# Latent-attention masks as 32-by-32 tiles of TensorE

## The chip, the cores and the metric

The kernel runs on one core of a Trainium2 chip. The core has a matrix engine (TensorE, PE in the profile; its weight loads have a row of their own, PEld), a vector engine (DVE), an activation engine (ACT), a general engine (POOL) and a queue for transfers (SP). Matrix products are written to PSUM, which this program uses as eight banks of 128 partitions by 512 float32 values. The metric is the device time of one execution in microseconds: 1879.91 us, the median of three runs (1879.69 to 1884.78).

## The reference

`x` has 8 sequences of 512 tokens with 128 channels. Two feed-forward stages with local attention stand around one attention over a latent space:

```python
x = x + 0.5 * ffn(layernorm(x))            # two layers each: local attention and a gated MLP
x = x + latent_attention(layernorm(x))     # 16 heads of 8 channels, causal
x = x + 0.5 * ffn(layernorm(x))
```

What bears on the change is the middle line, for each of 8 sequences and 16 heads:

```python
attn = einsum('bhql,bkl->bhqk', q_lat, c_kv) / sqrt(hs)
causal = tril(ones((T, T), bool))
attn = softmax(where(causal, attn, -inf))
```

The mask acts inside the 128-by-128 blocks on the diagonal of the 512-by-512 scores; blocks above the diagonal are not computed at all.

## The kernel before

The program has three parts: `ffn("f0")`, `latent_attention()`, `ffn("f1")`. In the two feed-forward parts every instruction is dealt out by the planner `Plan`, which orders steps by written costs and ranks while the program is being built. `latent_attention()` is written out in order by hand, and `in_order` keeps PE in that order. Some latent work lies outside its own part: `latent_begins` (inside f0, the last steps) makes the maxima of sequence 0 and of two batches of sequence 1, and `latent_ends` (inside f1, the first steps) makes the sums of sequence 7.

**Heads.** Sixteen heads are laid out as 4 groups `g` of 32 partitions by 4 heads `j` along the free dimension. A head's queries and keys fill 8 of its 32 partitions, the ninth carries a row for the shift by the maximum, and the rest is zero. A score product therefore contracts over 32 partitions, `rows = quadrant(g)`, and gives 128 output partitions.

**Units.** A unit is one PSUM bank (128 by 512). `maximum_products` (lines 1281 to 1304) puts one or two query blocks of scores into a bank, and DVE takes the row maximum (`maximum`, lines 1310 and 1314). `sum_products` (lines 1337 to 1362) puts the transposed scores into a bank, and ACT takes the exponential (`sum_exponential`, line 1366). `MAXIMA` and `SUMS` list which blocks share a bank. One block of 512 columns fills a bank, or two blocks do whose columns add up to 512.

**Masks.** Each unit begins by writing the mask into its diagonal blocks through PE, and the score products accumulate on top. Four matmuls, one for each 32 rows `k` of a diagonal block, take a piece of `masks["rows_of"]` as the stationary matrix (32 rows by 128 columns, of which 32 columns are an identity and the rest zero) and a piece of `masks["causal"]` or `masks["causal_t"]` as the moving one (lines 1288 and 1346). A piece writes all 128 output partitions, and adds zero on 96 of them. Only the first piece clears the bank (`start=(k == 0)`). The products come next: lines 1297 and 1355, float32, which the machine runs as two passes of weight load and matmul each.

**Pairs.** In the hand-ordered part the loop goes over `b` (7 sequences), the 10 batches of `SUMS` and the 4 head groups `g`. Each turn makes one sum unit of group `g` and, where one is left, one maximum unit of the next sequence of group `(g + 2) % 4`; `by_turns` interleaves the two units' matmuls one by one. This is called a pair here. There are 280 pairs, 272 of them with both units. All eight banks are given out in turn (`unit_bank`). In `latent_begins` and `latent_ends` two units of the same kind, of neighbouring groups, stand together: 24 and 20 such groups.

**Between the pairs** stand the value products (line 1372: 28 times 16 products over 128 partitions that write 32 partitions each), the transposes of their results (line 1453), and the projections of later sequences (lines 1421, 1426, 1434), at four fixed places of each sequence.

At the start of the program POOL builds the constants: `ident`, `ident16`, two bands, and the three masks (lines 317 and 325).

Of the kernel before, what the change touches and what calls it, by code (L numbers as in the profile page):

```python
# [12 lines left out]
ALU = mybir.AluOpType  # L13
# [3 lines left out]
P = 128  # L17
# [171 lines left out]
def kernel(  # L189
# [97 lines left out]
    ident16 = const.tile([P, P], BF16, name="ident16")  # L287
# [4 lines left out]
    for first in (True, False):  # L292
        band = const.tile([P, P], BF16, name=f"band{int(first)}")
        nc.gpsimd.memset(band, 0.0)
        for half in (0, WIN):
            rows = band[half : half + WIN]
# [14 lines left out]
    def quadrant(g):  # L311
        return slice(32 * g, 32 * g + 32)

    masks = {}
    for name in ("rows_of", "causal", "causal_t"):
        masks[name] = const.tile([P, 4, P], BF16, name=name)
        nc.gpsimd.memset(masks[name], 0.0)
    for g in range(4):
        for name, pattern, sign, op, fill in (
            ("rows_of", [[-32, 4], [1, P]], -1, ALU.not_equal, 1.0),  # L320
            ("causal", [[32, 4], [-1, P]], 1, ALU.is_ge, MASKED),
            ("causal_t", [[-32, 4], [1, P]], -1, ALU.is_ge, MASKED),
        ):
            rows = masks[name][quadrant(g)]
            nc.gpsimd.affine_select(
                out=rows, in_=rows, pattern=pattern, compare_op=op, fill=fill, base=0,
                channel_multiplier=sign,
            )
# [79 lines left out]
    def ffn(tagname, last):  # L408
# [600 lines left out]
        def latent_begins():  # L1009
# [67 lines left out]
            for b, held in [(0, held) for held in MAXIMA] + [(1, held) for held in MAXIMA[:LEAD]]:  # L1077
                q, kk = head_slots["q", b], head_slots["k", b]
                m = maxima_of(b)
                for half in (0, 1):  # L1080
                    banks = [Slot(mm), Slot(mm)]
                    units = [
                        (2 * half + n, lambda n=n, banks=banks: banks[n].tile) for n in range(2)
                    ]
                    step(
                        "lm", PE, 1.3, k,
                        lambda b=b, held=held, units=units: by_turns(
                            [maximum_products(b, held, g, bank) for g, bank in units]
                        ),
                        [(q, "d"), (kk, "d")], banks, [q, kk] + banks, 0.1,  # L1090
                    )
                    for (g, bank), t in zip(units, banks):
                        step(
                            "lr", DVE, 0.63, k,
                            lambda m=m, held=held, g=g, bank=bank: maximum(m, held, g, bank()),
                            [t], [("max", b, g)], [t], 0.0,
                        )
# [8 lines left out]
        def latent_ends():  # L1106
# [46 lines left out]
            for held in SUMS:  # L1153
                tiles, needs, slots = {}, [], []
                for half in (0, 1):
                    bank = Slot(pairs)
                    hold = [Slot(r_pT), Slot(r_pT)] if half else [Slot(r_pr)]
                    step(
                        "ep", PE, 1.3, k,
                        lambda held=held, half=half, bank=bank: by_turns([  # L1160
                            sum_products(b, held, 2 * half + n, lambda n=n: bank[:, n])
                            for n in range(2)
                        ]),
                        [(q, "d"), (kk, "d")], [bank], [q, kk, bank], 0.1,
                    )

                    def exponentials_(half=half, bank=bank, hold=hold, tiles=tiles):
                        if half:
                            for n in range(2):
                                tiles[2 + n] = flat(hold[n].tile)  # L1170
                                sum_exponential(tiles[2 + n], bank[:, n])
                        else:
                            t = flat(hold[0].tile)
                            sum_exponential(t.rearrange("p (n w) -> p n w", n=2), bank.tile)
                            tiles[0], tiles[1] = t[:, :512], t[:, 512:]

                    step(
                        "ee", ACT, 1.1, k, exponentials_, [bank], [(bank, 1)], [bank] + hold, 0.1
                    )
                    needs.append((bank, 1))  # L1180
                    slots += hold
# [38 lines left out]
    def heads(name, b):  # L1220

        if name == "v":
            return head_slots["v", b % 2].tile.rearrange("p n (h d) -> p n h d", d=32)
        if b % 3 == 2:
            half = slice(0, B // 2) if name == "q" else slice(B // 2, B)
            return Y[:, half].rearrange("p b n c -> p b (n c)")
        return head_slots[name, b % 3].tile
# [53 lines left out]
    def maximum_products(b, held, g, bank):  # L1281
        rows = quadrant(g)
        qp, kp = heads("q", b), heads("k", b)
        i0 = held[0][0][0]
        blocks = bank().rearrange("p (n w) -> p n w", w=P)
        diag = {3: blocks[:, 3:], 2: blocks[:, 2:], 1: blocks[:, 1::2]}[i0]
        todo = [
            lambda k=k: nc.tensor.matmul(
                diag[:, :, 32 * k :], lhsT=masks["rows_of"][rows, k],
                rhs=masks["causal"][rows, k, 32 * k :].unsqueeze(1)  # L1290
                .to_broadcast([32, len(held), P - 32 * k]),
                start=(k == 0), stop=False, skip_group_check=True,
            )
            for k in range(4)
        ]
        todo += [
            lambda i=i, j=j, at=at, n=n: nc.tensor.matmul(  # L1297
                bank()[:, at : at + (i + 1) * P], lhsT=qp[rows, j, i * P : (i + 1) * P],
                rhs=kp[rows, j, : (i + 1) * P],
                start=False, stop=(n == len(held) - 1), skip_group_check=True,  # L1300
            )
            for n, ((i, j), at) in enumerate(held)
        ]
        return todo
# [32 lines left out]
    def sum_products(b, held, g, bank):  # L1337

        rows = quadrant(g)
        qp, kp = heads("q", b), heads("k", b)  # L1340
        c0 = held[0][0][0]

        blocks = bank().rearrange("p (n w) -> p n w", w=P)
        diag = {0: blocks[:, :1], 1: blocks[:, ::3], 2: blocks[:, ::2]}[c0]
        todo = [
            lambda cut=cut, k=k: nc.tensor.matmul(
                diag[:, :, :cut], lhsT=masks["rows_of"][rows, k],
                rhs=masks["causal_t"][rows, k, :cut].unsqueeze(1)
                .to_broadcast([32, len(held), cut]),
                start=(k == 0), stop=False, skip_group_check=True,  # L1350
            )
            for k, cut in enumerate((32, 64, 96, 128))
        ]
        todo += [
            lambda c=c, j=j, at=at, n=n: nc.tensor.matmul(  # L1355
                bank()[:, at : at + T - c * P],
                lhsT=kp[rows, j, c * P : (c + 1) * P], rhs=qp[rows, j, c * P :],
                start=False, stop=(n == len(held) - 1), skip_group_check=True,
            )
            for n, ((c, j), at) in enumerate(held)  # L1360
        ]
        return todo
# [32 lines left out]
    def latent_attention():  # L1395
# [75 lines left out]
        for b in range(B - 1):  # L1471
            parts = {}
            for s, held in enumerate(SUMS):
                other = ahead.pop(0) if ahead else None
                tiles = {}
                for half in (0, 1):
                    two = two_tiles()
                    for n in range(2):
                        g = 2 * half + n
                        bank = unit_bank(f"st_{b}")  # L1480
                        units = [sum_products(b, held, g, lambda bank=bank: bank)]
                        if other is not None:
                            mb, mheld = other
                            mbank = unit_bank(f"sc_{mb}")
                            units.append(
                                maximum_products(mb, mheld, (g + 2) % 4, lambda mbank=mbank: mbank)
                            )
                        by_turns([
                            [lambda ins=ins: in_order(ins()) for ins in unit] for unit in units
                        ])  # L1490
                        sum_exponential(two[n], bank)
                        tiles[g] = two[n]
                        if other is not None:
                            maximum(maxima_of(mb), mheld, (g + 2) % 4, mbank)
# [124 lines left out]
```

## Time and profile before

| What | Value |
|---|---|
| Median of three runs | 1879.91 us |
| Profiled execution, its own time | 1883.39 us |
| Its span, first to last instruction | 1881.6 us |
| PE, share of the span busy | 93% |
| PE weight loads | 63% |
| DVE / ACT / POOL | 73% / 74% / 53% |
| Mean granted TensorE clock | 0.98 |
| Latent part, all eight banks in turn | about 823 to 1108 us of the span |
| Mask matmuls, each with a weight load | 2560 |

A row of a group reads: line, engine, operation, written tile, read tiles, shape, count, then the time in which any of the group was busy, the mean of one in ns, and the idle time of the engine just before them with what ended it. For PE a shape such as `32*128 32x256 bf16` says: 32 rows by 128 columns of stationary matrix, and 256 columns streamed past it. A float32 matmul has two rows in the records, one for each pass. Ends of matmuls are modelled and several are in flight at once, so the starts tell the pace, and a PE that is busy all the time need not be at its peak. The clock that TensorE was granted is told for each stretch of time.

### The profile page before, as it was taken

Reading aid. Unit: us, or ns where it says so; the run is one execution under the profiler, and the core shown is the slowest. Engines: PE = TensorE matmul, PEld = TensorE weight load, DVE = VectorE, ACT = ScalarE, POOL = GpSimd, SP = SyncE. Lnnn points to the kernel's source line nnn. Section 1 sums busy time; section 2 is a strip of 40 time slices with the busy share of each in tenths; the row PEclk is TensorE's granted clock in tenths of the full one; section 3 lists DMA queues with packets and bytes.
Section 4 is the critical chain, followed back from the end, with each engine's and each line's share of the span. In section 5 each row is a group of like instructions: output and inputs, shape, how many; then the busy total and the mean of one; then the engine's idle time right before and its main releaser. Section 6 shows DMA issues by size and latency. Waiting matters only on the chain.

```text
span 1881.6 us, 50927 instructions
## 1 busy us (share of the span) xinstructions
PE 1757.7 (93%) x19860; PEld 1179.0 (63%) x19860; DVE 1373.7 (73%) x2884; ACT 1389.6 (74%) x3911; POOL 990.1 (53%) x1685
## 2 busy tenths in 40 slices
PE   4899999999999989899999998989999999999998
PEld 2556666666666666467777764666666666666665
DVE  6888887777777867666766746878877777777764
ACT  2888878888888777236666666878888788778885
POOL 5776766666666665100000005867766666666651
PEclk9999999999999999769999999999999999999999
DMA  3111111111111111000000000111111111111110
GB/s 105 45 38 30 29 24 24 24 27 24 24 24 30 24 24 22 26 10 19 15 16 15 15 3 18 27 23 25 26 25 27 24 25 29 30 29 35 29 33 24
DMA packets 51968, 50.04 MB, mean 27 GB/s; under 512 B 22758, under 2 KB 34704, under 8 KB 51728
## 3 DMA queue, kind: packets, MB, share of 16 engines
q1 hardware_dynamic: 51584, 46.00, 10.5%
q8 instruction: 158, 2.59, 0.6%
q14 instruction: 82, 0.67, 0.1%
q10 hardware_dynamic: 144, 0.79, 0.1%
HBM read 6.30 MB, written 2.10 MB: 4 GB/s over the span
## 4 chain that ended last, share of the span: by engine, by line
PE 56%; DVE 18%; ACT 14%; POOL 6%; issue 4%; DMA 1%; SPq 1%; ACTq 0%; DVEq 0%; POOLq 0%
PE mm_f L542 9%; PE mm_f L504 8%; ACT pr_f L692 5%; PE mm_f L849 5%; PE st L1355 4%; PE mm_f L891 4%; PE mm_f L758 4%; PE mm_f L782 3%; PE lo L1372 3%; PE sc L1297 3%; DVE c_f L552 3%; DVE s_f L555 3%; PE sc_f L675 3%; ACT sq_f L568 2%; PE mm_f L1297 2%
## 5 line engine op out<-in xcount | busy, mean ns | idle before, releaser
L692 ACT ACTIVATE pr_f<-sc_f,nm_f,q_f 128x128 f32<-128x128 f32 x1024 | 460.3, 475 | 5.5 <-DVE nm_f L685 5.1
L542 PE MATMUL mm_f<-wqkv,hT_f 128*128 128x512 f32 x768 | 391.3, 613 | 30.4 <-DVE s_f L555 14.0
L576 POOL TENSOR_TENSOR qk_f<-c_f,s_f 128x512 f32<-128x512 f32 x256 | 325.0, 1274 | 115.1 <-DVE s_f L555 112.8
L700 POOL TENSOR_TENSOR pr_f<-pr_f,rso_f 128x512 f32<-128x512 f32 x256 | 266.0, 1040 | 220.8 <-DVE rso_f L716 180.7
L552 DVE TENSOR_TENSOR c_f<-mm_f,tab 128x512 f32<-128x512 f32 x256 | 175.3, 685 | 79.0 <-PE mm_f L542 34.6
L692 ACT ACTIVATION_READ_ACCUMULATOR pr_f<-sc_f,nm_f,q_f 128x1 f32 x1024 | 226.4, 221 | 0.0
L568 ACT ACTIVATE sq_f<-mm_f 128x512 f32<-128x512 f32 x256 | 153.1, 608 | 87.4 <-DVE s_f L555 61.4
L1366 ACT ACTIVATE pl<-st 128x512 f32<-128x512 f32 x280 | 152.8, 597 | 73.9 <-PE st L1355 59.8
L849 PE MATMUL mm_f<-fT_f,w 128*128 128x512 f32 (+1 forms) x384 | 190.5, 611 | 8.9 <-ACT ge_f L855 7.0
L504 PEld LDWEIGHTS mm_f<-ident,qk_f 128*128 128x128 f32 x1024 | 114.7, 141 | 128.9 <-POOL qk_f L612 52.1
L504 PE MATMUL mm_f<-ident,qk_f 128*128 128x128 f32 x1024 | 160.0, 280 | 31.8 <-POOL qk_f L612 12.8
L542 PEld LDWEIGHTS mm_f<-wqkv,hT_f 128*128 128x128 f32 x768 | 125.0, 192 | 99.1 <-issue 42.0
L684 DVE TENSOR_REDUCE nm_f<-sc_f 128x8 f32<-128x1024 f32 x128 | 155.3, 1214 | 42.6 <-PE sc_f L675 42.5
L758 PEld LDWEIGHTS mm_f<-pT_f,V_f 128*64 128x64 f32 (+1 forms) x4096 | 147.4, 136 | 60.2 <-issue 13.1
L758 PE MATMUL mm_f<-pT_f,V_f 128*64 128x64 f32 (+1 forms) x4096 | 179.8, 230 | 0.7 <-ACT pT_f L738 0.7
L555 DVE TENSOR_TENSOR s_f<-mm_f,tab 128x512 f32<-128x512 f32 x256 | 174.0, 680 | 0.0
L1387 POOL TENSOR_TENSOR X<-X,lon 128x128 f32<-128x128 f32 x26 | 11.9, 456 | 306.2 <-DVE lon L1381 306.2
L504 PE MATMUL mm_f<-ident,pr_f 128*128 128x128 f32 x1024 | 155.9, 280 | 11.5 <-DVE u_f L880 3.0
L504 PEld LDWEIGHTS mm_f<-ident,pr_f 128*128 128x128 f32 x1024 | 116.3, 142 | 74.1 <-POOL pr_f L700 33.0
L600 DVE TENSOR_REDUCE rn_f<-sq_f 128x16 f32<-128x1024 f32 x128 | 153.7, 1201 | 7.5 <-ACT sq_f L568 7.5
L782 PEld LDWEIGHTS mm_f<-wo,oT_f 128*128 128x128 f32 x1024 | 127.7, 191 | 43.0 <-ACT oT_f L771 18.1
L782 PE MATMUL mm_f<-wo,oT_f 128*128 128x128 f32 x1024 | 140.7, 280 | 3.2 <-ACT oT_f L771 2.9
(166 smaller groups left out, 3865.2 us busy)
## 6 DMA issues: line engine op xcount, KB each, us to landing
V_f<-V_f SPq DMA_DIRECT2D x224, 128.0 KB
hs_f<-Y SPq DMA_DIRECT2D x32, 112.0 KB
X<-in_x_dram SPq DMA_DIRECT2D x8, 256.0 KB
out_dram<-hs_f SPq DMA_DIRECT2D x8, 256.0 KB
Y<-fl SPq DMA_DIRECT2D x32, 32.0 KB
kT_f<-fl SPq DMA_DIRECT2D x32, 32.0 KB
V_f<-fl SPq DMA_DIRECT2D x32, 32.0 KB
wqkv<-in_wqkv_dram ACTq DMA_DIRECT2D x1, 768.0 KB
```

The costliest lines, as they stand in the source:

```text
L504: nc.tensor.transpose(dst[:, i * P : (i + 1) * P], src(i), ident)
L542: nc.tensor.matmul(ps.tile, lhsT=hT[:, i * P : (i + 1) * P], rhs=wqkv_sb[l][:, at * INNER : (at + 1) * INNER], start=True, stop=True,)
L552: nc.vector.tensor_mul(c1.tile, psv, tabs[l][:, 2 * s, i].unsqueeze(1).to_broadcast([P, H, DH]))
L555: nc.vector.tensor_mul(s1.tile.rearrange("p h (t d) -> p h t d", t=2), psv.rearrange("p h (t d) -> p h t d", t=2)[:, :, ::-1], tabs[l][:, ...
L568: lambda s=s, ps=ps: nc.scalar.activation(sq[:, s], ps.tile, AF.Square),
L576: lambda s=s, c1=c1, s1=s1: nc.gpsimd.tensor_add(qk[:, s].rearrange("p (h d) -> p h d", d=DH), c1.tile, s1.tile),
L684: nc.vector.tensor_reduce(nm.tile, sv, AX.X, ALU.max, negate=True)
L692: nc.scalar.activation(pr[:, h], sv[:, h % 2, h // 2], AF.Exp, bias=nm[:, h % 2, h // 2 : h // 2 + 1], scale=q8[:, h : h + 1], accum_out=s ...
L700: nc.gpsimd.tensor_mul(pr[:, heads], pr[:, heads], inv[:, heads].unsqueeze(2).to_broadcast([P, H // 2, P]),)
L758: nc.tensor.matmul(o[r * DH : (r + 1) * DH, u * P + w * WIN : u * P + (w + 1) * WIN], lhsT=(V2, V)[w][keys, i, h * DH : (h + 1) * DH], rhs ...
L782: nc.tensor.matmul(pw[:, :C], lhsT=oT[:, pr], rhs=wo_sb[l][:, pr], start=(pr == 0), stop=(pr == INNER // P - 1),)
L849: nc.tensor.matmul(ps[: hsz[c], :], lhsT=w1_sb[l][:, at + c * P : at + c * P + hsz[c]], rhs=fT.tile, start=True, stop=True,)
```

## The change

The stationary matrix of a mask piece becomes the 32-by-32 diagonal block of the bfloat16 identity (`ident16[rows, rows]`), and the piece writes only the 32 partitions that are its own (`diag[quadrant(k), ...]`). As the pieces no longer share partitions, each clears its own part of the bank (`start=True`). `masks["rows_of"]` and the POOL instructions that fill it are gone. The order of the instructions on PE, ACT and SP and the waits among them stay as they are; the number of matmuls and of weight loads stays too. DVE has the same work, with a few small instructions of one layer norm in another order.

```diff
-    for name in ("rows_of", "causal", "causal_t"):
+    for name in ("causal", "causal_t"):
         masks[name] = const.tile([P, 4, P], BF16, name=name)
         nc.gpsimd.memset(masks[name], 0.0)
     for g in range(4):
         for name, pattern, sign, op, fill in (
-            ("rows_of", [[-32, 4], [1, P]], -1, ALU.not_equal, 1.0),
...
             lambda k=k: nc.tensor.matmul(
-                diag[:, :, 32 * k :], lhsT=masks["rows_of"][rows, k],
+                diag[quadrant(k), :, 32 * k :], lhsT=ident16[rows, rows],
                 rhs=masks["causal"][rows, k, 32 * k :].unsqueeze(1)
                 .to_broadcast([32, len(held), P - 32 * k]),
-                start=(k == 0), stop=False, skip_group_check=True,
+                start=True, stop=False, skip_group_check=True,
             )
...
             lambda cut=cut, k=k: nc.tensor.matmul(
-                diag[:, :, :cut], lhsT=masks["rows_of"][rows, k],
+                diag[quadrant(k), :, :cut], lhsT=ident16[rows, rows],
                 rhs=masks["causal_t"][rows, k, :cut].unsqueeze(1)
                 .to_broadcast([32, len(held), cut]),
-                start=(k == 0), stop=False, skip_group_check=True,
+                start=True, stop=False, skip_group_check=True,
             )
```

## The prediction

> **What bounds the kernel now.** First the page, by slices, to see whether PE is at its limit where the masks are.
>
> ```profile
> PE   4899999999999989899999998989999999999998
> PEclk9999999999999999769999999999999999999999
> ```
>
> A slice is 47 us; the latent part is slices 17 to 24. PE is busy throughout, and the clock dips only in slices 17 and 18. Next, windows cut at the latent part's edges, then the value products (line 1372) alone in the long one.
>
> ```profile
> core 0: us, PE busy (x) PEld busy (x) DVE busy (x) ACT busy (x) POOL busy (x), PEclk, DMA share, GB/s
> 771.50:822.90 51.40, 47.60 (x363) 33.33 (x362) 38.21 (x92) 3.20 (x10) 1.80 (x1) 0.57 0.04 8
> 822.90:1108.50 285.60, 285.60 (x5077) 206.34 (x5076) 189.31 (x386) 183.03 (x337) 11.85 (x26) 0.99 0.05 15
> 1108.50:1143.40 34.90, 33.07 (x440) 18.06 (x435) 8.06 (x36) 23.30 (x39) 3.86 (x13) 1.00 0.01 2
> ...
> 822.90:1108.50 285.60, 65.48 (x886) 25.41 (x886) 0.99 0.05 15
> ```
>
> The same query by lines 1453, 1426, 1434, 1421 and 1325 gives 17.06, 11.90, 6.95, 4.39 and 2.09 us. With the 65.48 that is 107.9 us that belong to no pair; 285.6 - 107.9 = 177.7 us are left for 280 pairs, 0.635 us a pair. DVE's maxima stand 0.60 us apart, start to start, in every run of pairs (the timeline has 7 in 4.28 us), so a pair is now paced by DVE, with PE close behind.
>
> How PE does a pair in that time shows in the timeline (start, length, engine, line).
>
> ```profile
> 959.95 1.16 PE L1372 MATMUL lo<-pl,V_f 128*32 128x384 f32 x20
> 961.03 1.12 PE L1426 MATMUL pq<-xT,full_q 128*128 128x512 f32 x2
> 962.00 1.02 PE L1426 MATMUL pq<-xT,full_k 128*128 128x512 f32 x2
> 962.95 0.18 PE L1346 MATMUL st<-causal_t,rows_of 32*128 32x32 bf16 x1
> 962.96 0.28 PE L1288 MATMUL sc<-causal,rows_of 32*128 32x256 bf16 x1
> ...
> 963.12 0.64 PE L1355 MATMUL st<-kT_f,V_f 32*128 32x512 f32 x1
> ...
> 963.24 0.56 PE L1297 MATMUL sc<-V_f,kT_f 32*128 32x384 f32 x1
> 963.25 0.18 PE L1346 MATMUL st<-causal_t,rows_of 32*128 32x32 bf16 x1
> 963.25 0.28 PE L1288 MATMUL sc<-causal,rows_of 32*128 32x256 bf16 x1
> ...
> 963.60 0.59 PE L1355 MATMUL st<-kT_f,V_f 32*128 32x512 f32 x1
> ```
>
> Two readings carry the forecast. The second pair's masks start at 963.25, while the first pair's products (963.12 and 963.24) have just begun: as long as the shape is 32 rows by 128 columns, four row groups run side by side, two pairs at once. And where the shape changes, nothing overlaps. The weight-load rows at those places:
>
> ```profile
> 961.03 0.30 PEld L1426 LDWEIGHTS pq<-xT,full_q 128*128 128x128 f32 x2 [0.41 <-issue]
> ...
> 962.95 0.09 PEld L1346 LDWEIGHTS <-rows_of 32*128 32x128 bf16 x1 [0.76 <-issue]
> ```
>
> The value products end at 959.95 + 1.16 = 961.11 and the projections at 962.00 + 1.02 = 963.02; the next load starts 0.07 us before each end, though inside one shape a load starts beside the running matmul. I find the same 0.07 at every place in the trace where rows or columns go from one of 32, 64 and 128 to another, some 860 of them, also where only the columns change (128*128 to 128*32, 27 places). It leaves some 95 ns between the last streamed column and the next load.
>
> [...]
>
> **The change, part by part.**
>
> *Shape.* Masks become 32*32, products stay 32*128. Each pair, and each of the 24 + 20 groups outside, now has two changes of shape where it had none: into the masks, and into the products. This decides.
>
> *A pair after, at full clock.* Masks: two units' eight pieces go to eight different tiles. The nearest row is the local attention's own mask (line 665, four pieces of shape 64*64, 4 in 0.41 us with 0.40 each), so pieces start 3.5 ns apart; eight take 0.03. The last ends after 0.27 (256 columns, line 1346) and the products' load starts 0.07 earlier: 0.22 us. If column tiles of one row group did not run side by side, it would be as now, about 0.36. Products: the first load is no longer covered. In the projections at 961.03 the two passes start 0.53 apart behind a change and 0.43 apart elsewhere, so 0.107 is bare. The streams total 512 columns in two passes, 0.427 each: 0.853 (split units stream as much). Then 0.095 until the next pair's load. Sum 0.22 + 0.107 + 0.853 + 0.095 = 1.27 us, and the next pair can't start under it. Against 0.635: 280 x 0.635 = +178 us. With DVE at 0.60 and ACT at 0.60 a pair, PE alone now paces; their waits for PE grow, and none of them is late.
>
> *The clock.* It halves at 770.2 and at 787.3. What ran just before the second, 783.9 to 787.3, where two groups' maxima stand:
>
> ```profile
> L1297 PE MATMUL mm_f<-V_f,kT_f 32*128 32x512 f32 x8 | 2.4, 657 | 0.0
> L1288 PE MATMUL mm_f<-causal,rows_of 32*128 32x128 bf16 x4 | 0.8, 211 | 1.0 <-DVE lnm L1314 1.0
> ```
>
> Weighted by the share of the array's cells, 8 passes x 0.427 / 4 are 0.85 us, and 1280 mask columns at 0.43 ns / 4 are 0.14: 0.29 of the window. Counted so in 3.41 us windows over the whole trace, the clock falls after windows of 0.08 to 0.37, stays at 0.40 and more (once at 0.33), and comes back after 0.80 or more (not at 0.62). A pair after the change has 0.853 x 2 / 4 = 0.427 plus 0.03 of small masks in 1.27 us: 0.36, now about 0.8. So the stage comes to the edge of the clock. Windows with a value product in them are well above, windows of pairs alone vary from about 0.32 to 0.39. At half clock the streams and loads double: 0.33 + 0.213 + 1.707 + 0.095 = 2.34 us, +1.07 a pair, at 0.38 of the cells, so it stays down until the next value products (28 of them, 10 pairs apart). Bounds: 0 if it never falls; at the most three pairs in ten are at full clock behind each value product, 196 x 1.07 = 210, and a third of the other 108 us doubles, 35: +245. I take about the middle, 112 pairs at half: +120.
>
> *Groups outside.* In `latent_begins` the clock is 0.50; DVE's maxima (four starts, 789.75 to 795.00) put three groups in 5.25 us, 1.75 each. After: 2.34. Some 18 of the 24 stand back to back: +10 (0 to 14). In `latent_ends` 20 groups lie among other shapes; one alone costs 0.03 more, one that overlapped its neighbour 0.62: +6 (1 to 12).
>
> *Weight loads.* 2560 of 92 to 96 ns (128 columns) become 32 columns; the nearest row is line 1372's 32-column load, 109 ns. They lie beside matmuls except after a change of shape, where the first is in the 0.22. Bounds -13 to +16 ns a group: nothing. If the cover goes, 324 groups x 0.016 = 5 us.
>
> *Clearing and waits.* `start=True` on every piece is what line 665 does; no cost shows there. No wait is added or taken, on PE, ACT, SP or POOL.
>
> *POOL at the start.* One fill (0.47 start to start) and four selects (0.59) go, 2.8 us. The first layer norm's small steps start on POOL at 14.28 when its queue is empty, though their input was there at 8.54. So the first projections (18.44) come earlier, unless a load is late next: -3 (-3 to 0).
>
> *Sum*, against the profiled execution's 1883.4 us (span 1881.6 and 1.8 around it): +178 + 120 + 10 + 6 - 3 = +311, 2194. The median lies 3.5 lower: 2190.
>
> **Rivals.**
> 1. *The drain comes, the clock holds.* For it: one window at 0.33 did not drop it, and pairs alone average 0.36. Against: one low window is enough, and each stretch has several. 1880 + 178 + 13 = about 2070; with less bare time a pair (1.22) 2055.
> 2. *The drain holds back only the row group concerned.* For it: row groups of one shape run freely. Against: at 962.95 the load waits for the whole array, though there the array was one tile, so the trace doesn't decide. Two pairs overlap, 1.27 / 2 = 0.635: no change in the pairs, about 1880 to 1900.
> 3. *Other side: faster.* 32*32 beside 32*128 is no change of shape for the machine. Column tiles then shorten the masks and DVE alone paces: (0.635 - 0.600) x 280 = 10, and 3 at the start: 1867. It decides as soon as a pair takes less than 0.635. Against: 128*128 to 128*32 differs in columns alone and drains all 27 times.
>
> **How the numbers follow.** Forecast (drain, clock falls in a part) 0.62; rival 1 0.24; rival 2 0.07; rival 3 0.07. Rivals 2 and 3 are left out of the range. Low end: rival 1 at 1.22 a pair and the lower bounds, 1880 + 164 - 3 = 2041, so 2040. High end: 1880 + 178 + 245 + 14 + 12 - 3 = 2326, so 2320. Faster by over 0.3% (about what a measurement of this kernel tells from no change): rival 3, 0.07. Rival 2 is split: 0.03 same, 0.04 slower. Slower: 0.90.
>
> **What would show it.** Masks of 32*32 at 4 ns spacing; PEld loads of the products 0.07 us before the last mask's end; no mask start while a product runs; pair to pair 1.27 us at clock 1.0 and 2.34 at 0.5; DVE's maxima as far apart, with idle time put down to PE; the clock row below 9 in slices of the latent part; both feed-forward parts as long as before. Masks starting beside the other row groups' products, or maxima still 0.60 apart, would prove the drain wrong; a clock row of nines would prove the +120 wrong.

## The result and the profile after

The changed kernel takes 2286.11 us, the median of four runs (2272.50 to 2293.17), against 1881.21 us (1879.69 to 1884.78) for the kernel before: a ratio of 1.214, with a 95% interval of 1.2115 to 1.2166. The profiled execution is the shortest of the four, 2272.5 us with a span of 2270.7 us. It is 389.1 us longer than the span of before, and every figure below is taken from these two profiled executions.

All line numbers after the constants are one lower than before: masks L1345 and L1287, products L1354 and L1296, value products L1371. First the same two rows of the page by slices; a slice is now 57 us.

```profile
PE   5999999999999899999999999998999999999998
PEclk9999999999999856766676666689999999999999
```

The latent part is slices 14 to 27, fourteen where there were eight shorter ones, and the clock row is between 5 and 8 in all of them. Before, it dipped in two. The PE row gives no hint: it is at nines. The windows cut at the first mask of each stretch say how much each took, and the last row counts the value products (L1371) alone.

```profile
core 0: us, PE busy (x) PEld busy (x) DVE busy (x) ACT busy (x) POOL busy (x), PEclk, DMA share, GB/s
767.40:825.80 58.40, 55.29 (x362) 26.90 (x362) 38.12 (x92) 2.15 (x9) 1.80 (x1) 0.59 0.03 6
825.80:1496.00 670.20, 669.40 (x5095) 352.35 (x5094) 214.73 (x387) 198.16 (x338) 11.76 (x26) 0.66 0.02 6
1496.00:1529.50 33.50, 33.50 (x382) 15.55 (x380) 7.26 (x34) 21.48 (x35) 3.29 (x12) 1.00 0.01 2
...
825.80:1496.00 670.20, 104.16 (x896) 33.73 (x896) 0.66 0.02 6
```

Measured from mask to mask in the same way, the edges of the three stretches of before lie at 771.5, 822.9, 1111.4 and 1140.5 us. The long stretch of before reads:

```profile
822.90:1111.40 288.50, 287.77 (x5097) 207.73 (x5097) 189.57 (x387) 183.64 (x338) 11.85 (x26) 0.99 0.05 15
```

That gives the whole bill:

| Stretch | Before, us | After, us | Difference |
|---|---|---|---|
| Start to first maximum mask | 771.5 | 767.5 | -4.0 |
| `latent_begins`, first maximum mask to first sum mask | 51.4 | 58.4 | +7.0 |
| Hand-ordered part, to the first mask of `latent_ends` | 288.5 | 670.2 | +381.7 |
| `latent_ends`, first mask to last mask | 29.1 | 33.5 | +4.4 |
| Rest, to the end | 741.1 | 741.2 | 0 |

In the hand-ordered part PE is busy for 669.4 of 670.2 us. DVE's and ACT's busy times grow by only 25 and 15 us (189.6 to 214.7, and 183.6 to 198.2), and both now wait. Two groups of the page show on what; the last number of the mean is in ns, and behind the bar stand the idle time and what ended it.

```profile
L1365 ACT ACTIVATE pl<-st 128x512 f32<-128x512 f32 x280 | 167.2, 597 | 399.2 <-PE sc L1296 367.4
L1309 DVE TENSOR_REDUCE lnb<-sc 128x4 f32<-128x512 f32 x112 | 77.5, 692 | 210.7 <-PE sc L1296 210.7
```

The work itself still takes 597 and 692 ns. ACT waits 399 us ahead of its exponentials, nearly all for PE.

How a pair runs now is in PE's timeline. The clock falls at 961.95, so the pair whose masks start at 961.09 runs almost wholly at full clock and the next one at half (start, length, engine, line).

```profile
960.56 0.59 PE L1354 MATMUL st<-kT_f,V_f 32*128 32x512 f32 x1
960.78 0.38 PE L1296 MATMUL sc<-Y 32*128 32x128 f32 x2
961.09 0.20 PE L1345 MATMUL st<-causal_t,ident 32*32 32x64 bf16 x1
...
961.11 0.20 PE L1287 MATMUL sc<-causal,ident 32*32 32x64 bf16 x1
961.32 0.58 PE L1354 MATMUL st<-kT_f,V_f 32*128 32x384 f32 x1
...
962.40 0.41 PE L1296 MATMUL sc<-Y 32*128 32x128 f32 x1
962.75 0.23 PE L1345 MATMUL st<-causal_t,ident 32*32 32x64 bf16 x1
...
962.76 0.39 PE L1345 MATMUL st<-causal_t,ident 32*32 32x256 bf16 x1
962.77 0.23 PE L1287 MATMUL sc<-causal,ident 32*32 32x64 bf16 x1
963.08 1.00 PE L1354 MATMUL st<-kT_f,V_f 32*128 32x384 f32 x1
...
964.75 0.42 PE L1296 MATMUL sc<-Y 32*128 32x128 f32 x1
965.09 0.23 PE L1345 MATMUL st<-causal_t,ident 32*32 32x64 bf16 x1
```

Eight masks start within 0.02 us, so the column tiles do run side by side. Then nothing starts until they are through, the products run, and the next pair's masks start only when these are through: 961.09 to 962.75 to 965.09, 1.66 us across the fall of the clock and 2.34 us below it. The two pairs that overlapped before (masks at 962.95 and again at 963.25) no longer do. The weight loads at the two changes of shape:

```profile
963.08 0.28 PEld L1354 LDWEIGHTS st<-kT_f,V_f 32*128 32x128 f32 x1 [0.22 <-issue]
963.09 0.28 PEld L1296 LDWEIGHTS sc<-Y 32*128 32x128 f32 x1
...
965.09 0.10 PEld L1345 LDWEIGHTS <-ident 32*32 32x32 bf16 x1 [0.22 <-issue]
```

The last mask ends at 962.76 + 0.39 = 963.15 and the products' load starts 0.07 before; the last product ends at 964.75 + 0.42 = 965.17 and the load for the next masks starts some 0.07 before. The masks at 965.09 belong to other row groups than the products that end there, and still wait. These rows decide between the forecast and rival 2: the drain, the wait at a change of shape for all that still runs, takes the whole array. The trace of after has 605 changes between these two shapes, and at every one the load starts 71 to 73 ns before the last matmul's end.

DVE's maxima show the pair as a pace.

```profile
959.97 0.69 DVE L1309 TENSOR_REDUCE lnb<-sc 128x4 f32<-128x512 f32 x1 [3.13 <-PE sc L1296]
961.24 0.69 DVE L1309 TENSOR_REDUCE lnb<-sc 128x4 f32<-128x512 f32 x1 [0.58 <-PE sc L1296]
962.88 0.69 DVE L1309 TENSOR_REDUCE lnb<-sc 128x4 f32<-128x512 f32 x1 [0.95 <-PE sc L1296]
965.23 0.69 DVE L1309 TENSOR_REDUCE lnb<-sc 128x4 f32<-128x512 f32 x1 [1.66 <-PE sc L1296]
967.58 0.69 DVE L1309 TENSOR_REDUCE lnb<-sc 128x4 f32<-128x512 f32 x1 [1.65 <-PE sc L1296]
```

1.27 us from start to start at full clock, 2.35 at half. Over the part the median is 1.28 (88 intervals wholly at full clock) and 2.35 (131 wholly at half). Between 862.9 and 1494.4 the clock falls 27 times; it is typically full for 6.8 us and half for 10 to 24 us. Each time that it came back in this part, value products had run in the 3.5 us before.

### The profile page after: what moved, and what is told of

Its sections match the earlier page's. It is cut to its first block, busy times and chain, and to the rows that moved or that the text cites. A ratio compares the mean times of both kernels' runs of the same rounds, so it can differ in the third digit from the quotient of the medians.

```text
span 2270.7 us, 50918 instructions
## 1 busy us (share of the span) xinstructions
PE 2153.1 (95%) x19860; PEld 1317.2 (58%) x19860; DVE 1397.9 (62%) x2884; ACT 1401.9 (62%) x3911; POOL 985.3 (43%) x1680
## 4 chain that ended last, share of the span: by engine, by line
PE 66%; DVE 13%; ACT 10%; POOL 6%; issue 4%; DMA 1%; SPq 0%; ACTq 0%; DVEq 0%; POOLq 0%
PE st L1354 16%; PE mm_f L541 8%; PE mm_f L503 7%; PE mm_f L848 5%; PE lo L1371 5%; ACT pr_f L691 4%; PE sc L1296 4%; PE mm_f L890 3%; PE mm_f L757 3%; PE mm_f L781 3%; PE sc_f L674 2%; DVE c_f L551 2%; DVE s_f L554 2%; ACT sq_f L567 2%; PE mm_f L1296 2%
## 5 line engine op out<-in xcount | busy, mean ns | idle before, releaser
L1365 ACT ACTIVATE pl<-st 128x512 f32<-128x512 f32 x280 | 167.2, 597 | 399.2 <-PE sc L1296 367.4
L1354 PE MATMUL st<-kT_f,V_f 32*128 32x128 f32 (+3 forms) x640 | 324.0, 632 | 0.0
L1296 PE MATMUL sc<-V_f,kT_f 32*128 32x384 f32 (+3 forms) x624 | 315.2, 633 | 0.0
L1313 DVE TENSOR_REDUCE lnm<-sc 128x1 f32<-128x512 f32 (+1 forms) x160 | 110.7, 692 | 176.8 <-PE sc L1296 160.6
L1309 DVE TENSOR_REDUCE lnb<-sc 128x4 f32<-128x512 f32 x112 | 77.5, 692 | 210.7 <-PE sc L1296 210.7
L757 PEld LDWEIGHTS mm_f<-pT_f,V_f 128*64 128x64 f32 (+1 forms) x4096 | 147.4, 136 | 60.2 <-issue 14.1
L1354 PEld LDWEIGHTS st<-kT_f,V_f 32*128 32x128 f32 x640 | 142.0, 251 | 60.0 <-issue 34.1
```

The lines of the kernel that those rows point to most:

```text
L757: nc.tensor.matmul(o[r * DH : (r + 1) * DH, u * P + w * WIN : u * P + (w + 1) * WIN], lhsT=(V2, V)[w][keys, i, h * DH : (h + 1) * DH], rhs ...
L1296: lambda i=i, j=j, at=at, n=n: nc.tensor.matmul(bank()[:, at : at + (i + 1) * P], lhsT=qp[rows, j, i * P : (i + 1) * P], rhs=kp[rows, j, : ...
L1354: lambda c=c, j=j, at=at, n=n: nc.tensor.matmul(bank()[:, at : at + T - c * P], lhsT=kp[rows, j, c * P : (c + 1) * P], rhs=qp[rows, j, c * ...
```

## The experiments

The theory has two steps. Each change of shape makes TensorE wait until the whole array is empty, so that pairs no longer overlap; and the work that is left fills too few of the array's cells to hold the clock. The rivals: that small masks or clearing each piece cost the time by themselves, that the clock falls for another reason, that only the row group concerned waits.

### Half as many changes of shape

```diff
+                    units, read = [], []
                     for n in range(2):
                         g = 2 * half + n
                         bank = unit_bank(f"st_{b}")
-                        units = [sum_products(b, held, g, lambda bank=bank: bank)]
+                        units.append(sum_products(b, held, g, lambda bank=bank: bank))
+                        read.append(lambda n=n, bank=bank: sum_exponential(two[n], bank))
...
-                        by_turns([
-                            [lambda ins=ins: in_order(ins()) for ins in unit] for unit in units
-                        ])
-                        sum_exponential(two[n], bank)
...
+                    by_turns([
+                        [lambda ins=ins: in_order(ins()) for ins in unit] for unit in units
+                    ])
+                    for r in read:
+                        r()
```

The masks stay 32 by 32; the maxima of the two pairs are put into `read` in the same way. Four units instead of two stand between two changes of shape, in four different row groups.

> The changed kernel, with the masks of two pairs issued together and then the products of the two pairs, so that four units share the two changes of shape. Nothing else changes: the same pieces of 32 by 32, the same clearing, the same number of matmuls. Theory (each change of shape empties TensorE, and nothing overlaps across it): a group of two pairs takes 0.25 + 0.107 + 0.853 + 0.095 = 1.31 us in place of 2 x 1.28, 0.65 a pair, and the share of cells doubles to about 0.7, so the clock stays at 1.0 through the latent part. The hand-ordered part takes about 140 x 1.31 + 108 = 291 us against 288 before; the whole 1885 to 1925 us (some waits for banks included). Rival (the narrow pieces or their clearing are slow in themselves): as many pieces, so near 2286 us. Rival (the drain is of one row group alone): no gain from sharing, near 2286 us.

Measured: 1912.37 us (1903.57 to 1930.01), a ratio of 1.018 (1.0115 to 1.024). The windows from mask to mask:

```profile
768.60:828.00 59.40, 56.78 (x362) 27.40 (x362) 38.23 (x92) 2.03 (x9) 1.80 (x1) 0.56 0.03 6
828.00:1130.60 302.60, 301.21 (x5103) 172.10 (x5102) 198.62 (x387) 182.78 (x338) 11.92 (x26) 0.98 0.05 14
1130.60:1175.00 44.40, 44.40 (x389) 19.14 (x388) 7.24 (x33) 21.66 (x35) 3.31 (x12) 0.73 0.00 1
```

The hand-ordered part falls from 670.2 to 302.6 us with the same masks and the same matmuls. The clock is full from 837.8 to 1134.8 without a break, and maxima stand 0.61 us apart inside a group of two pairs and mostly 0.7 to 0.9 from group to group. So neither the small masks nor their clearing cost the time; where they stand does. Of the 36.6 us by which the span is still longer than before, 14.1 lie in this part, 8.0 in `latent_begins`, which was not regrouped, and 15.3 in `latent_ends`, in which the clock was at half from 1134.8 to 1158.7; the start is 2.9 earlier and the rest 2.1 longer.

The same grouping in the kernel before is the control:

> The kernel before, with the masks of two pairs together and then their products, as in the other run with two pairs; masks of 32 by 128. It tells what the grouping alone does. Theory: no change of shape stands between pairs here, so grouping has nothing to save: within 1% of before, 1865 to 1900 us. If the grouping itself were a gain, this run would be clearly below 1865.

Measured: 1887.95 us (1885.75 to 1889.20), 1.0036 (1.0024 to 1.0049), the hand-ordered part 294.7 us against 288.5.

```profile
821.90:1116.60 294.70, 290.64 (x5097) 187.02 (x5096) 194.81 (x387) 182.38 (x338) 11.86 (x26) 0.99 0.05 14
```

Grouping alone gains nothing, so what it gave the changed kernel was the changes of shape that it took away, and the clock with them.

### More work, at a higher clock

```diff
+                        spare = unit_bank(f"sp_{b}")
+                        idle = quadrant((g + 1) % 4)
+                        units.append([None] * 4 + [
+                            lambda spare=spare, idle=idle: nc.tensor.matmul(
+                                spare, lhsT=heads("k", b)[idle, 0, :P],
+                                rhs=heads("q", b)[idle, 0], start=True, stop=True,
+                            )
+                        ])
...
```

> The changed kernel, with one product more in each pair: 512 columns, float32, on a row group that is idle then, into a spare bank that nobody reads. It streams beside the pair's products and takes no time of its own, but adds 0.21 us of a quarter of the cells twice, 0.36 to about 0.52 of the cells. Theory (the clock follows the share of cells that stream): the clock stays at 1.0 in the latent part, pairs take 1.28 us throughout, and the whole takes about 1881 + 280 x 0.645 + 7 = 2065 us (2050 to 2090), some 220 us less than the changed kernel in spite of more work. Rival (the clock falls because of the empty stretches at each change of shape, which stay as they are): 2286 us or a little more.

Measured: 2085.83 us (2084.10 to 2087.55), 1.109 (1.1066 to 1.111): 200 us less than the changed kernel, with a product more in every pair. The windows of the whole hand-ordered part, and of the stretch in which the clock stayed full:

```profile
828.00:1311.90 483.90, 483.10 (x5657) 272.19 (x5656) 212.43 (x387) 198.09 (x338) 11.92 (x26) 0.95 0.03 9
865.20:1298.70 433.50, 433.50 (x5331) 246.72 (x5324) 200.34 (x360) 185.88 (x316) 11.92 (x26) 1.00 0.04 10
```

The clock is full for 433.5 us on end. The maxima there show the drain without the clock:

```profile
984.39 0.69 DVE L1313 TENSOR_REDUCE lnm<-sc 128x1 f32<-128x512 f32 x1 [0.60 <-PE sp L1490]
985.68 0.69 DVE L1313 TENSOR_REDUCE lnm<-sc 128x1 f32<-128x512 f32 x1 [0.60 <-PE sp L1490]
986.97 0.69 DVE L1313 TENSOR_REDUCE lnm<-sc 128x1 f32<-128x512 f32 x1 [0.60 <-PE sp L1490]
```

1.29 us a pair, twice what a pair took before, and the profile puts each maximum's wait down to the spare product of line 1490, the last to end. This run parts the two terms: the changes of shape keep the pair at 1.28, and the clock is what took the pairs of the changed kernel from 1.28 to their mean of 1.83. A share of cells explains it, 0.36 a pair without the spare product and (3 x 0.853 / 4 + 0.03) / 1.28 = 0.52 with it. Counted from the records in windows of 3.41 us, each pass's stream time weighted by its rows and columns over 128 x 128 (all times at full or half clock in this part are multiples of it: 3.4, 6.8, 10.2, 13.7 us and so on), the changed kernel's clock falls behind windows of 0.21 to 0.36 and holds behind windows from 0.35 up; with the spare product the windows of the full stretch are at 0.49 and more, but for its end, where one of 0.41 holds and one of 0.34 is followed by the fall. PE's busy time does not explain it: 669.4 of 670.2 us at clock 0.66, 483.1 of 483.9 at 0.95. Nor does PE's idle time: the changed kernel's part has 0.8 us of it in all, and the clock falls 27 times there.

### Half the pieces changed

```diff
-                diag[:, :, 32 * k :], lhsT=masks["rows_of"][rows, k],
+                diag[quadrant(k), :, 32 * k :], lhsT=ident16[rows, rows],
...
-                start=(k == 0), stop=False, skip_group_check=True,
+                start=True, stop=False, skip_group_check=True,
```

This is the kernel before with the change in the maximum units alone; the masks of the sum units stay at 128 columns.

> The kernel before with the change made to the maximum units alone; the sum units keep masks of 32 by 128. Since a pair interleaves the two units' pieces one by one, nearly every mask piece of a pair now follows one of the other shape. Theory (price per change of shape, 0.1 us behind each stream): the masks of a pair take their streams one after another, 1024 columns or 0.43 us, and 8 x 0.1 us, 1.23 in place of 0.22; a pair takes about 1.23 + 0.107 + 0.853 + 0.095 = 2.28 us at full clock, at 0.24 of the cells, so the clock falls as well, and a pair takes about 3.7 us at half clock. With a third of the pairs at full clock the whole is 1881 + about 750 = 2630 us (2400 to 2850). Rival (each changed piece costs something of its own): half of the pieces, half of the loss, near 2080 us.

Measured: 2658.84 us, a single execution, beside 1879.87 for the kernel before; it lies in the range of the theory.

```profile
829.40:1888.40 1059.00, 1058.24 (x5095) 540.39 (x5094) 215.00 (x387) 197.53 (x338) 11.75 (x26) 0.58 0.01 4
```

PE's timeline at full clock, where a pair's masks now go one by one:

```profile
963.02 0.18 PE L1346 MATMUL st<-causal_t,rows_of 32*128 32x32 bf16 x1
963.13 0.23 PE L1288 MATMUL sc<-causal,ident 32*32 32x128 bf16 x1
963.29 0.20 PE L1346 MATMUL st<-causal_t,rows_of 32*128 32x64 bf16 x1
...
963.99 0.18 PE L1288 MATMUL sc<-causal,ident 32*32 32x32 bf16 x1
964.10 0.69 PE L1355 MATMUL st<-kT_f,V_f 32*128 32x512 f32 x1
```

Half of the masks are small, and the loss is almost twice as large. In a pair the two units are interleaved piece by piece, so a 32-column mask now stands next to a 128-column one, and there are eight changes of shape to a pair instead of two (2176 in the trace, 272 pairs). Maxima stand 2.03 or 2.17 us apart at full clock (19 intervals, 2.28 expected) and mostly 3.5 to 3.77 at half. It is the changes that are paid for, not the small pieces.

### No change of shape at all

```diff
-            lambda i=i, j=j, at=at, n=n: nc.tensor.matmul(
-                bank()[:, at : at + (i + 1) * P], lhsT=qp[rows, j, i * P : (i + 1) * P],
+            lambda i=i, j=j, at=at, n=n, k=k: nc.tensor.matmul(
+                bank()[quadrant(k), at : at + (i + 1) * P],
+                lhsT=qp[rows, j, i * P + 32 * k : i * P + 32 * k + 32],
...
-            for n, ((i, j), at) in enumerate(held)
+            for n, ((i, j), at) in enumerate(held) for k in range(4)
```

The products of the sums are cut in the same way, so that everything in a unit is 32 by 32.

> The changed kernel, with the score products in the same shape as the masks: each product's stationary matrix is cut into four of 32 columns, and each piece writes its own 32 partitions. Four times as many product matmuls and loads, but no change of shape inside or between pairs. Theory (change of shape): pairs overlap again and DVE paces at 0.60 us; the masks' pieces run side by side, so PE needs less than before: 1865 to 1890 us. Rival (narrow pieces are slow in themselves): worse than the changed kernel, since there are more of them, above 2286 us.

Measured: 1969.40 us (1962.75 to 1971.92), 1.046 (1.0441 to 1.0486). The direction held, 317 us less than the changed kernel; the number did not.

```profile
817.60:1194.80 377.20, 373.87 (x10423) 255.10 (x10422) 209.98 (x387) 195.32 (x338) 11.84 (x26) 0.99 0.05 13
```

The clock is full but for the first microseconds, and a pair takes (377.2 - 109.0) / 280 = 0.96 us (109.0 us is what the lines that belong to no pair take in this part of the kernel before). PE's timeline has the next pair's masks beside the running products:

```profile
960.64 0.27 PE L1355 MATMUL st<-Y 32*32 32x128 f32 x1
960.66 0.20 PE L1346 MATMUL st<-causal_t,ident 32*32 32x64 bf16 x1
...
960.70 0.25 PE L1346 MATMUL st<-causal_t,ident 32*32 32x192 bf16 x1
960.73 0.37 PE L1296 MATMUL sc<-V_f,kT_f 32*32 32x256 f32 x1
...
961.02 0.21 PE L1287 MATMUL sc<-causal,ident 32*32 32x128 bf16 x1
```

With one shape the overlap is back, as the theory says. But the masks come in two portions, 0.3 us apart, at this place, and the pair is not at DVE's pace. Two more runs ask why. The first groups two pairs as above:

> The kernel in which products too are cut into pieces of 32 columns, now with the units of two pairs issued together, four row groups in turn. Question: why did the kernel with one shape everywhere take 0.99 us a pair and not 0.60. Theory (the pieces of one pair, some 34 matmuls with as many loads, fill the queue in front of TensorE while they wait for their own tiles, so the next pair's pieces for idle row groups come too late): with four row groups in turn the queue holds work for the whole array, a pair comes down to 0.60 to 0.65 us, and the whole to 1860 to 1895 us. Rival (a narrow piece is slow in itself, for its loads or for streams that disturb each other): as many pieces, so near 1969 us.

Measured: 1937.61 us (1936.05 to 1940.43), 1.031 (1.0294 to 1.0323). It fits neither expectation.

```profile
818.00:1167.30 349.30, 331.35 (x10431) 195.49 (x10430) 199.15 (x387) 182.49 (x338) 11.88 (x26) 1.00 0.05 14
```

Maxima stand 0.61 apart inside a group, with a gap behind it, and a pair takes (349.3 - 109.0) / 280 = 0.86 us. The second cuts into 64 columns, masks as well as products, and starts from the kernel before:

```diff
-                diag[:, :, 32 * k :], lhsT=masks["rows_of"][rows, k],
+                diag[half(k // 2), :, 32 * k :],
+                lhsT=masks["rows_of"][rows, k, half(k // 2)],
...
-                start=(k == 0), stop=False, skip_group_check=True,
+                start=(k % 2 == 0), stop=False, skip_group_check=True,
...
-                bank()[:, at : at + (i + 1) * P], lhsT=qp[rows, j, i * P : (i + 1) * P],
+                bank()[half(k), at : at + (i + 1) * P],
+                lhsT=qp[rows, j, i * P + 64 * k : i * P + 64 * k + 64],
```

Here `half(k)` is the range of 64 partitions from 64 k on, and a product becomes two; the sums are cut in the same way.

> The kernel before with every piece of a unit, masks and products, cut into tiles of 32 rows by 64 columns: no change of shape between masks and products, masks over half the partitions, twice as many products. It asks what kept the version with 32-column pieces everywhere at 0.96 us a pair. If it is the number of matmuls with their weight loads (in that run 33.3 mask and product matmuls a pair in 0.96 us, 29 ns each), this one has 20.6 a pair, 0.60 us, no more than DVE's maxima take: a pair stays at 0.60 to 0.65, the hand-ordered part at 280 to 292 us, the whole at 1865 to 1890. If narrow pieces cost something by themselves, in proportion to the cuts, the pair lies between 0.65 and 0.96, about 0.75, and the whole at 1900 to 1930. On whether the changed kernel pays for its changes of shape this run says nothing unless the pair goes beyond 1.2 us, which would speak against it.

Measured: 1878.64 us (1874.87 to 1880.51), 0.9969 (0.9954 to 0.9984).

```profile
823.00:1107.00 284.00, 282.83 (x6870) 199.11 (x6870) 190.15 (x386) 183.66 (x338) 11.90 (x26) 0.99 0.06 16
```

Maxima are 0.60 apart again. So narrower pieces don't cost in proportion to the cuts: in these runs twice as many products are free, with DVE the slower one, and four times as many are not. That fits a price of about 29 ns for each matmul with its load (20.6 a pair here, 33.3 with 32 columns), but a price of the 32-column pieces alone would look the same, and the grouped version's 0.86 us, 26 ns for each of as many matmuls, is explained by neither. This stays open.

### A version faster than both

If the share of cells sets the clock, spare work should help the kernel before as well, where it runs at half clock from 787.3 to 828.2, in `latent_begins`. There two idle row groups get a product each beside every group of maxima; the results are not read.

```diff
+            def spares(b, g, spare, n):
+                rows = quadrant(g)
+                return [None] * 4 + [
+                    lambda: nc.tensor.matmul(
+                        spare[:, n], lhsT=heads("k", b)[rows, 0, :P],
+                        rhs=heads("q", b)[rows, 0], start=True, stop=True,
+                    )
+                ]
...
                             [maximum_products(b, held, g, bank) for g, bank in units]
+                            + [spares(b, 2 - 2 * half + n, spare, n) for n in range(2)]
...
```

> The kernel before (masks of 32 by 128), with two spare products of 512 columns beside each group of maxima in the first feed-forward part, on the row groups that are idle then, into banks that nobody reads. There the clock fell to a half from 787 to 828 us. Theory (the clock follows the share of cells): the window before the fall rises from 0.29 to about 0.5, the second fall does not come, groups of maxima go from 1.75 us to DVE's 1.25, and the kernel takes 5 to 12 us less than before: 1869 to 1876 us. Rival (the spare products only cost time, the clock is set otherwise): 1881 to 1900 us.

Measured: 1870.78 us (1869.75 to 1872.48), 0.9952 (0.9938 to 0.9965).

```profile
770.70:814.10 43.40, 36.75 (x458) 23.32 (x457) 37.60 (x92) 1.90 (x9) 1.80 (x1) 0.91 0.04 8
```

The stretch takes 43.4 us instead of 51.4. The clock is at half until 771.5 and from 781.7 to 788.5, and full from then to the end of the stretch. So the second fall did come, against the expectation: the 3.41 us window before it, from 778.3, still had a share of only 0.20 of the cells. It lasted 6.8 us instead of 41. The same spare products, as two pieces of 64 columns each, go with the version of 64 columns:

```diff
-                    lambda: nc.tensor.matmul(
-                        spare[:, n], lhsT=heads("k", b)[rows, 0, :P],
+                    lambda k=k: nc.tensor.matmul(
+                        spare[64 * k : 64 * k + 64, n], lhsT=heads("k", b)[rows, 0, 64 * k : 64 * k + 64],
...
+                    for k in range(2)
```

> The version with tiles of 32 rows by 64 columns for masks and products, with the spare products of the beginning added (two for each group of maxima, on idle row groups, here also as tiles of 64 columns, so that no shape changes; their results are not read). With 64-column tiles alone the beginning still runs at half clock from 784.2 to 828.6 and takes 50.6 us; with the spare products the kernel before needed 43.4 there, at full clock from 788.5 on. If the share of the array's cells at work sets the clock, the two gains add: 1878.6 less 8 to 10, and a little less waiting in the hand-ordered part, 1866 to 1872, a ratio of 0.990 to 0.995 and below both versions. If the smaller masks leave too few cells at work for the same spare products, the clock stays at half in the beginning and the time is that of the 64-column tiles alone, 1876 to 1881, or more.

Measured: 1866.96 us (1866.27 to 1869.47), 0.9929 (0.9916 to 0.9943), the fastest of all.

```profile
769.80:810.90 41.10, 32.65 (x700) 18.05 (x700) 37.52 (x92) 1.86 (x9) 1.80 (x1) 0.99 0.04 10
```

With 64 columns alone the same stretch reads:

```profile
772.50:823.00 50.50, 44.08 (x506) 23.41 (x506) 38.13 (x92) 2.02 (x9) 1.80 (x1) 0.60 0.03 8
```

From first maximum mask to first sum mask it is 41.1 us against 50.5, at a clock of 0.99 against 0.60. The two gains add. The 64-column tiles are also the way in which smaller masks do pay here, by 0.3%: cut the products alike, and nothing changes shape between masks and products.

## Why the prediction was right, and where its sizes were off

**The direction and the mechanism held.** 2286 us lies in the range of 2040 to 2320, near its upper end, and 96 us above the 2190 forecast. Against the profiled execution, on which the sum was made, it is 389 measured against 311. That execution is the shortest of the four: the median one is 14 us longer, at a mean clock of 0.877 against 0.884, so there the clock's term is larger still than below.

**The drain, +178 forecast.** It held. A pair was forecast at 1.27 us at full clock and 2.34 at half, and measured 1.28 and 2.35; its first part, from the masks' load to the products' load, at 0.22 and 0.33, and measured 0.23 and 0.34. The reading of before on which it rests was right but for a detail: of 868 changes of shape in that trace, 58 have the load later than 0.07 us before the end, and none has it earlier. With the stretch cut at the first mask of `latent_ends`, a pair before is (288.5 - 109.0) / 280 = 0.641 us, where 109.0 is the busy time of the other lines in that window, and the term is (1.27 - 0.641) x 280 = 176.

**The clock, +120 forecast. This is the mis-sized term.** The other lines of the hand-ordered part (value products 104.16, transposes 28.97, the rest 25.36) now take 158.5 us, 49.5 more than before, since they too run partly at half clock. The pairs take (670.2 - 158.5) / 280 = 1.828 us, 0.558 above 1.27, which is 156 us. The clock therefore cost 156 + 49 = 205 us, 85 above the forecast and inside its bounds of 0 and 245. The clock row gives the same by another way: it is at half for 457 us of the part, and there a pair loses 1.07 of its 2.34 us, which makes 209. The forecast took 112 pairs at half clock, "about the middle" between never and the most; 156 / 1.07 is 146. And the slowing of the other work stood in the upper bound (35 us) but was left out of the value taken. The middle was chosen between two ends because the trace of before has only a few windows near 0.36, some with a fall and some without. The working itself had the sharper argument, in what it held against rival 1: one low window is enough, and each stretch has several (in the trace of before, the window up to 681.5 has 0.28 of the cells, the one ahead of it 0.86, and the clock falls). That speaks for the upper end. In the trace of after, windows between 0.35 and 0.36 go either way, and pairs alone give 0.34 to 0.37.

**The groups outside, +10 and +6 forecast:** +7.0 and +4.4, both within their bounds. **POOL's start, -3 forecast:** -4.0, a little beyond the bound of -3. The start scatters by more than that excess: in the profiled executions it takes 769.8 to 772.5 us in the six kernels that still fill `rows_of`, and 766.0 to 768.6 in the five that don't. **Weight loads and clearing, nothing:** the small pieces' loads take 0.10 us, and the grouped version, which has every one of them, takes 302.6 us for the hand-ordered part where the same grouping with masks of 128 columns takes 294.7. So they cost at most those 8 us, in which its changes of shape are counted too. The rest of the kernel, 741.1 and 741.2 us, is unmoved.

The sum by these terms: 176 + 205 + 7.0 + 4.4 - 4.0 = 388, against 389.1. It closes by construction, since the clock's 205 is what the drain left over; the 209 from the clock row is the independent check.

**The rivals.** Rival 1, drain without the clock, is what the spare products made of the kernel, and there its size held: 2085.83 us against about 2070, with the clock still at half at both ends of the part. Rival 2 falls by the loads at 965.09, which wait for other row groups' products. Rival 3 falls by the same rows: 32 by 32 beside 32 by 128 is a change of shape. What in the profile was named as the sign of each came about: masks 3 to 4 ns apart, loads 0.07 before the end, no mask beside a product, a clock row below nine throughout.

## What to carry to other kernels

Before cutting matmuls into smaller tiles, look in the trace at what overlaps now across row groups, and count the changes of shape, in columns as well as rows, that the cut puts in: here two a pair cost each pair 0.64 us of lost overlap though the masks themselves became shorter. If a small tile is wanted, cut its neighbours to the same shape or gather several units' masks ahead of their products (here 1878.64 us in 64-column tiles and 1912.37 us with two pairs together, against 2286.11). Weigh each stretch by the share of array cells that stream as well as by PE's busy time, and where it comes near the 0.35 at which the clock fell here, price the half clock at its upper end, other work in that stretch included; a spare product on idle rows can be cheaper than the clock (here 200 us less, with one in each pair).

## What the runs showed of the hardware that was not expected

- Adding work made kernels shorter: 200 us with a spare product in each pair of the changed kernel, and 9 us (0.9952) with spare products in 43 us of the kernel before.
- The clock can swing for hundreds of microseconds with PE always busy: 27 falls in 632 us, mean 0.67.
- Cutting masks and products into pieces of 64 columns cost nothing (0.60 us a pair, twice the products), while pieces of 32 columns took 0.96 us with no change of shape and at full clock. The cause was not settled.
- Interleaving two shapes piece by piece is far worse than two changes a pair: 2.03 to 2.17 us a pair at full clock against 1.28, mostly 3.5 to 3.77 at half against 2.35.
